# A state space layer: tiles and order of the decays, and the rows of the step product

## The chip, the cores and the metric

The kernel runs on one core of a Trainium2 chip. The metric is the device time of one execution in microseconds (us). The profile shows one execution on that core. Its engines are TensorE (PE; its weight loads are PEld), VectorE (DVE), ScalarE (ACT), GpSimd (POOL) and SyncE (SP, which here issues DMAs). "q" behind an engine's name is its sequencer.

## The reference, cut to what matters

The model has four layers of a token mixer and a channel mixer on an input of 4 x 64 x 128 x 128 floats. The change lies in the mixer of the third layer alone, a state space model (Mamba) over 64 x 128 positions of 128 values, cut here to its core:

```python
xs = silu(conv(xi))                       # D_INNER = 128 channels, 16384 positions a batch entry
x_dbl = einsum('bld,ed->ble', xs, x_proj_w)
dt, Bm, Cm = x_dbl[..., :4], x_dbl[..., 4:20], x_dbl[..., 20:]
dt = softplus(einsum('blr,dr->bld', dt, dt_proj_w) + dt_proj_b)
A = -exp(A_log)                           # 128 channels x 16 states
def step(h, t):
    dt_t, B_t, C_t, x_t = t
    h = exp(dt_t[:, :, None] * A) * h + (dt_t * x_t)[:, :, None] * B_t[:, None, :]
    return (h, einsum('bds,bs->bd', h, C_t))
y = (scan(step) + xs * D) * silu(z)
```

An output projection, a two-layer GELU network and the residual follow.

## The kernel before

The layer is the function `l2_conv`. Positions are cut into 64 chunks of 512 positions for two batch entries: `chunks` holds two groups of 32. A chunk n has T = 32 **units**, 16 for each batch entry b; unit t works on 128 rows (two states of 64 channels) x 512 positions:

- `decay(t)` (L2824, ACT) makes da = exp(dt * A) in a ring of five SBUF tiles;
- `spread(t)` (L2834, PE), for each pair of units, spreads a row of B over the partitions of a PSUM bank (bs), and `inputs(t)` (L2868, DVE) multiplies it by dx = dt * x. There are four banks for this, and `spread` must wait until the scan that used its bank is done;
- `one_state(t)` runs the scan (L2876, DVE), then multiplies the result by C (gs, L2881, POOL);
- `summed(t)` (L2890 and L2892, PE) adds two units' gs into py.

Units 16 and 17 of each chunk stand **apart**: their da goes into a PSUM bank and POOL makes their input (L2862).

While chunk n is scanned, the following chunks are prepared and the last one is finished. All this is written into one list of turns by hand, and the engines' order is the order of the list (`manual_schedule`); each engine works in order. In turn t the list has first the decay of unit t + 3, then `spread` of t + 3 (where that is even), POOL's input of t + 5, the loads of C, `inputs` of t + 1, `one_state` of t, then the other steps put at turn t, and last `summed` of t - 5 in every second turn. Counted within a chunk, the steps that matter below are:

| turn | step |
|---|---|
| 24 to 28 | `conv` (PE, L2621), `conv_out` (ACT, L2633) for the next chunk |
| 30, 31, 1 | `gate_in` (PE, L2639), `gate_out` (ACT, L2642), `silu` (ACT, L2648, two table loads) |
| 30 to 6 | `norm` of a later chunk: `scale` (ACT, L2541), `centre` (PE, L2547), `square` (ACT, L2550 and L2551, turn 4), `mean2` (PE, L2556, turn 5), `root` (ACT) |
| 7, 8 | `bcr` (PE, L2654): 100 rows: three times the 32 rows of B and C, then the four step rows |
| 9 | `bcr_out` (ACT): copies to bt (96 rows, L2658), bc (64 rows, L2659), r (the four step rows, L2660); `c_out`, the DMA of bc to memory (cd) |
| 10 to 13 | `minus` (PE, L2669) and `part` (ACT, L2675), twice; `back` (PE, L2575) and `kept` (ACT, L2581) of `norm` |
| 9 to 14 | `project_out` (PE, L2753), `projected` (ACT, L2756) |
| 15 | `steps` (PE, L2680): dt_proj times r |
| 16 to 18 | `parts` (ACT, L2684 and L2685), `exp`, `one_more` (L2688 to L2693, which makes `less`), `log` (L2696) |
| 18 to 23 | four products on POOL (`lost` L2699 to `scaled` L2716) and the DMAs that lay out dt and dx (L2708) |
| 18 to 22 | `layer1` (PE, L2761) and `hidden` (ACT, L2766), for b = 0 at 18 and 19, for b = 1 at 21 and 22 |
| 24 | `gelu` (ACT, L2771, two table loads) |
| 28 to 33 | `layer2` (PE, L2777 to L2780) and `put` (ACT, L2787) |

Every four chunks, `statistics` is added: sixteen DVE instructions (L2495) at turns 7 to 22, a merge on POOL (turn 24), ACT's root (L2511, turn 26) and POOL's refinement (turn 28), which the `scale` of the next chunk waits for.

## Time and profile before

| | |
|---|---|
| median of 3 runs | 10706.98 us (10702.95 to 10707.34) |
| the profiled execution | 10710.25 us, span 10708.5 us, mean granted PE clock 0.774 |
| the layer's scans (L2876) | first start 5839.5 us, last start 9713.0 us of the span (its waits included) |
| stretch 5840 to 9714 us | PE 3392.8, DVE 3693.8, ACT 3172.6, POOL 3508.0 us busy of 3874.0; clock 0.89; DMA 0.49 |
| one scan, one input product | 1271 ns, 677 ns |
| one decay, one product by C | 715 ns, 1272 ns |

A line of the groups names the source line, the engine, the operation, what it writes and reads with shapes, how often; behind the bar its busy time and the mean of one, then how long the engine stood idle just before it and who ended that. "<-" points to what is read or waited for. A line of the timeline gives start and duration, in brackets the idle time before it and what ended it. A line of the waits gives the waiting engine and line, who it waited for, the total in us, how often, and the longest. A line of the table of stretches gives the stretch, its length, the busy time and number of instructions of each engine asked for, the clock that PE was granted (1.00 is full), the busy share of the DMA engines and GB/s. Successive DVE instructions overlap by about 0.09 us.

### The profile page before, as it was taken

To read this page: it belongs to the slowest core of one execution; us is meant where nothing else is said; L and a number is where in the kernel's file an instruction comes from. 1 tells how busy PE (TensorE), PEld (TensorE's weight loads), DVE (VectorE), ACT (ScalarE), POOL (GpSimd) and SP (SyncE) were. 2 spreads that over 40 slices of the span, in tenths; PEclk is the share of its full clock that TensorE was granted. 3 is DMA by queue.
4 is the path that set the end of the run, shared out by engine and by line. 5 is a ranking of instruction groups with operands and counts; after the bars stand their busy time and mean duration, and the time that the engine had idled before them with its cause. 6 is when DMAs were issued, how large, how long until landed. Compare 5 with 4: busy or idle time off the path is not lost. (4 is left out here: it accounts for less than half of the span.)

```text
span 10708.5 us, 115288 instructions
## 1 busy us (share of the span) xinstructions
PE 6421.0 (60%) x33010; PEld 3761.6 (35%) x33010; DVE 9037.8 (84%) x14995; ACT 7129.8 (67%) x10685; POOL 6791.7 (63%) x6142
## 2 busy tenths in 40 slices
PE   7888686000000000029997888888888888887664
PEld 5665454000000000028885333333333333335342
DVE  7577746999999999987774999999999999996555
ACT  4245443788886777655653888888888888885443
POOL 1000025899996777515553989899999999983322
PEclk8888798555555555559997888888889888888887
DMA  6322246111111222121111544445454454543544
GB/s 198 115 39 53 72 161 160 51 57 59 57 57 58 75 75 75 63 59 52 56 49 51 129 122 123 124 120 130 120 127 123 123 130 120 129 115 108 185 151 164
DMA packets 806496, 1080.38 MB, mean 101 GB/s; under 512 B 245612, under 2 KB 462926, under 8 KB 792270
## 3 DMA queue, kind: packets, MB, share of 16 engines
q1 hardware_dynamic: 761918, 946.59, 31.4%
q0 software_dynamic: 34368, 124.14, 3.5%
q8 instruction: 266, 4.36, 0.2%
q14 instruction: 392, 3.21, 0.1%
q10 hardware_dynamic: 9552, 2.08, 0.1%
HBM read 699.16 MB, written 255.91 MB: 89 GB/s over the span
## 5 line engine op out<-in xcount | busy, mean ns | idle before, releaser
L2881 POOL TENSOR_TENSOR gs<-hist,cc 128x512 f32<-128x512 f32 x2048 | 2569.9, 1272 | 274.5 <-DVE hist L2876 203.7
L2876 DVE TENSOR_TENSOR_SCAN hist<-da,state,bs 128x512 f32<-128x512 f32 x1860 | 2360.8, 1271 | 50.8 <-ACT da L2824 49.2
L1752 PE MATMUL pm<-ident,m 128*1 128x128 f32 x1 | 0.4, 372 | 2812.9 <-DMA pk<-spare 2812.9
L2868 DVE TENSOR_TENSOR bs<-dx,bs 128x512 f32<-128x512 f32 x1920 | 1300.3, 677 | 165.1 <-PE bs L2834 115.4
L1509 POOL TENSOR_TENSOR diff<-key 128x2048 f32<-128x2048 f32 (+11 forms) x364 | 1384.2, 3860 | 81.7 <-DVE key L1514 75.9
L2824 ACT ACTIVATE da<-dt,am 128x512 f32<-128x512 f32 x1920 | 1294.3, 715 | 36.8 <-DVE hist L2876 28.4
L2892 PE MATMUL py<-gs,both 128*64 128x512 f32 x4096 | 1210.0, 671 | 0.4 <-POOL gs L2881 0.2
L1752 PEld LDWEIGHTS pm<-ident,m 128*1 128x1 f32 x1 | 0.1, 79 | 2813.0 <-issue 2813.0
L1507 ACT COPY low<-key 128x2048 f32<-128x2048 f32 (+11 forms) x364 | 627.5, 1724 | 314.2 <-DVE key L1514 276.9
L1561 ACT ACTIVATE back<-turned 128x2048 int32<-128x2048 int8 (+6 forms) x546 | 626.1, 1165 | 308.9 <-DVE rank L1572 294.1
L1570 DVE COPY_PREDICATED rank<-back,rank 128x2048 int16<-128x2048 int32 (+6 forms) x546 | 787.8, 1478 | 19.3 <-ACT keep L1565 6.2
L1514 DVE TENSOR_TENSOR key<-low,key 128x2048 f32<-128x2048 f32 (+11 forms) x364 | 744.5, 2045 | 12.4
L1513 DVE TENSOR_TENSOR key<-low,key 128x2048 f32<-128x2048 f32 (+11 forms) x364 | 749.2, 2058 | 2.4 <-ACT low L1507 2.4
L1510 ACT ACTIVATE turned<-diff 128x2048 int8<-128x2048 f32 (+11 forms) x364 | 600.4, 1699 | 7.9 <-POOL diff L1509 7.9
L1555 POOL TENSOR_TENSOR both<-rank 128x1280 int32<-128x1280 int32 (+5 forms) x156 | 381.1, 2443 | 298.8 <-DVE rank L1572 170.8
L2303 PE MATMUL pe<-ew,xg 128*128 128x128 f32 x4096 | 509.9, 278 | 0.0
L2303 PEld LDWEIGHTS pe<-ew,xg 128*128 128x128 f32 x4096 | 495.2, 194 | 22.0 <-issue 3.9
L1031 POOL DMA_DIRECT2D state<-zz x16 | 18.5, 1156 | 763.0 <-DVE zz L1021 349.3
L1576 POOL TENSOR_TENSOR rank<-both,rank 128x256 int32<-128x256 int32 (+10 forms) x312 | 423.5, 1379 | 117.5 <-DVE rank L1570 89.4
L2834 PE MATMUL bs<-bt,pick 96*128 96x512 bf16 x960 | 394.8, 411 | 123.6 <-DVE hist L2876 120.9
L2761 PE MATMUL pa<-o,f 128*128 128x256 f32 x1024 | 362.5, 515 | 101.4 <-ACT gl L2766 81.6
L2892 PEld LDWEIGHTS py<-gs,both 128*64 128x64 f32 x4096 | 214.2, 142 | 594.0 <-issue 247.7
(860 smaller groups left out, 18030.7 us busy)
## 6 DMA issues: line engine op xcount, KB each, us to landing
cc<-cd SPq DMA_DIRECT2D x1024, 256.0 KB
xt<-state SPq DMA_DIRECT2D x64, 1024.0 KB
dt<-w SPq DMA_DIRECT2D x512, 128.0 KB
dx<-up SPq DMA_DIRECT2D x512, 128.0 KB
xo<-state SPq DMA_DIRECT2D x128, 256.0 KB
state<-xo POOLq DMA_DIRECT2D x128, 256.0 KB, 3.3
xl<-in_L_ffn_weight SPq DMA_DIRECT2D x32, 1024.0 KB
tk<-in_x SPq DMA_DIRECT2D x32, 512.0 KB
```

The source lines that it names most:

```text
L1507: nc.scalar.copy(c, l)
L1509: nc.gpsimd.tensor_sub(d, lo[part], hi[part])
L1513: nc.vector.tensor_tensor(lo[part], c, hi[part], ALU.min)
L1514: nc.vector.tensor_tensor(hi[part], c, hi[part], ALU.max)
L1561: nc.scalar.activation(m, sv[part], AF.Relu)
L1570: nc.vector.copy_predicated(l, m, h)
L2303: T.matmul(w["pe"][:, j, :], w["xg"][:, q, j, :], ew[:, q, :], start=False, stop=(j == 3 and q == E - 1))
L2824: nc.scalar.activation(da, x_["dt%d" % b][:, s % 2, :], AF.Exp, scale=am[:, s : s + 1])
L2868: nc.vector.tensor_mul(live["db", t], x_["dx%d" % b][:, s % 2, :], live["bs", t - s % 2])
L2876: nc.vector.tensor_tensor_scan(h, live.pop(("da", t)), live.pop(("db", t)), 0.0 if first else state[b][:, s : s + 1], ALU.mult, ALU.add,)
L2881: nc.gpsimd.tensor_tensor(gs, h, live.pop(("cc", t)), ALU.mult)
L2892: nc.tensor.matmul(x_["py%d" % b][h * H : h * H + H], both, live.pop(("gs", t - 1 + h)), start=False, stop=(s == S - 1),)
```

## The change

- `dtw`, the weights of the step product, gets 3N + R = 100 rows instead of R = 4: a memset to zero, and the DMA of the four true rows into the last ones.
- `bcr_out` makes two copies instead of three: bc takes all 100 rows, r is gone. `steps` multiplies all 100 rows of bc by the 100 rows of `dtw`; the first 96 meet zeros.
- The ring for da gets eight tiles instead of five.
- Decays of units that do not stand apart are issued five turns ahead instead of three, and still first in their turn. Those of the two units apart stay at three.

```diff
-        dtw = load("dtw", [R, D], prm["dt_proj_wT"])
+        dtw = cp.tile([3 * N + R, D], F32, name="dtw")
+        nc.vector.memset(dtw, 0.0)
+        nc.sync.dma_start(dtw[3 * N :], prm["dt_proj_wT"])
...
                 nc.scalar.copy(tile_of(x_, "bt", [3 * N, 2, L], dt=BF16), ps[0 : 3 * N])
-                nc.scalar.copy(tile_of(x_, "bc", [2 * N, 2, L], bufs=1), ps[0 : 2 * N])
-                nc.scalar.copy(tile_of(x_, "r", [R, 2, L], bufs=1), ps[3 * N : 3 * N + R])
+                nc.scalar.copy(tile_of(x_, "bc", [3 * N + R, 2, L], bufs=1), ps[0 : 3 * N + R])
...
-                    nc.tensor.matmul(pu[:, b, :], dtw, x_["r"][:, b, :], start=True, stop=True)
+                    nc.tensor.matmul(pu[:, b, :], dtw, x_["bc"][:, b, :], start=True, stop=True)
...
-            da = bank(t, t % 2) if apart(t) else sb.tile([P, L], F32, name="da", bufs=5)
+            da = bank(t, t % 2) if apart(t) else sb.tile([P, L], F32, name="da", bufs=8)
...
-                if 0 <= t + 3 < units:
+                if 0 <= t + 5 < units and not apart(t + 5):
+                    decay(t + 5)
+                if 0 <= t + 3 < units and apart(t + 3):
                     decay(t + 3)
```

## The prediction

> **What bounds the kernel now.** The change lies in one layer. Its scan line L2876 runs from 5840 us to 9714 us (first and last start in the view of that line), 64 chunks of 32 units, about 60.5 us a chunk. In the table of stretches VectorE is the busiest engine there:

> ```profile
> 7000.00:7500.00 500.00, 438.30 (x1741) 186.91 (x1740) 478.00 (x562) 412.01 (x622) 452.86 (x457) 0.89 0.50 125
> ```

> Columns: PE, PE loads, DVE, ACT, POOL busy, granted clock, DMA. DVE lacks 22 us of 500. Its waits over the layer:

> ```profile
> DVE bs L2868 <- PE bs L2834: 115.4, 110, 3.2
> DVE hist L2876 <- ACT da L2824: 50.5, 49, 3.1
> ```

> So 166 us wait for PE or ACT, and that is all the change can win. Next the DVE timeline, which shows where. The waits repeat every four chunks (statistics cover four), some 242.3 us: 3.06 us for da at unit 5 and 1.29 us at unit 10 of the first chunk (A), 1.98 us at A's unit 22, 1.47 and 1.26 us at unit 26 of the second and third (B, C), 0.2 to 0.4 us elsewhere; about 10.4 us in all, beside 231.9 us of DVE work.

> ```profile
> 8882.48 1.28 DVE L2876 TENSOR_TENSOR_SCAN hist<-da,state,bs 128x512 f32<-128x512 f32 x1 [3.05 <-ACT da L2824]
> ...
> 8890.95 0.69 DVE L2868 TENSOR_TENSOR bs<-dx,bs 128x512 f32<-128x512 f32 x1 [1.29 <-PE bs L2834]
> ...
> 8895.00 0.70 DVE L2868 TENSOR_TENSOR bs<-dx,bs 128x512 f32<-128x512 f32 x1 [0.40 <-PE bs L2834]
> ...
> 8913.68 0.69 DVE L2868 TENSOR_TENSOR bs<-dx,bs 128x512 f32<-128x512 f32 x1 [1.98 <-PE bs L2834]
> ```

> Why is PE late? Following PE and ACT in time through chunk B gives one unbroken loop: bcr product (PE, ends 7013.69), three copies (ACT, to 7016.67), minus to steps (PE, 7016.72 to 7025.48), parts to hidden(0) (ACT, 7025.58 to 7035.14), layer1(1) to spread(26) (PE, to 7041.06), layer2 (PE, to 7057.56), put, silu, square (ACT, to 7065.5), mean2, dself, spread(10), bcr. It takes 59 us, DVE's own chunk 56.9. The loop, not the number of da tiles, is the bound.

> PE's clock belongs to it. Cut into stretches of 3.41 us, the granted clock is 1.00 or 0.50, nothing between:

> ```profile
> 7018.84:7022.25 3.41, 3.41 (x32) 1.00 0.42 121
> 7022.25:7025.66 3.41, 3.41 (x11) 1.00 0.50 109
> 7025.66:7029.08 3.42, 3.34 (x8) 0.51 0.24 72
> 7029.08:7032.49 3.41, 3.41 (x15) 0.99 0.35 82
> 7032.49:7035.90 3.41, 1.29 (x6) 1.00 0.00 0
> 7035.90:7039.32 3.42, 3.42 (x8) 0.51 0.61 153
> ```

> A stretch with PE busy under some 45% (1.29 us) is followed by one at half clock. The second line is fully busy and is followed by half clock too; 1.98 us of it are the steps product L2680, which uses 4 of 128 rows. Over the layer, all 44 full-clock stretches that steps share with at most 0.42 of other PE work were followed by half clock, the 15 with 0.53 or more of other work by full clock. I read: four rows don't count as work. In chunk A this half clock makes layer1(0) 3.78 us instead of 1.99 and the product behind it 1.98 instead of 1.08, and so the 1.98 us wait at unit 22.

> **The change, part by part.**

> One copy less. The groups (busy us, mean ns, idle before and its releaser) show that the number of rows doesn't set a copy's time:

> ```profile
> L2669 PE MATMUL pa<-bt,minus_i 64*64 64x512 bf16 (+1 forms) x256 | 77.7, 383 | 58.8 <-ACT r L2660 58.2 <-ACT bt L2675 0.6
> ...
> L2658 ACT CAST bt<-pa 96x1024 bf16<-96x1024 f32 x64 | 64.5, 1007 | 226.2 <-PE pa L2654 226.2
> L2660 ACT COPY r<-pa 4x1024 f32<-4x1024 f32 x64 | 64.4, 1006 | 1.5
> L2659 ACT COPY bc<-pa 64x1024 f32<-64x1024 f32 x64 | 64.3, 1005 | 0.0
> ```

> So bc with 100 rows takes 1.005 us, r's 1.006 us goes, and the DMA to cd leaves as before. PE's minus waited 0.86 us a chunk for r (58.2 us in all); that goes, as project_out before it ends 0.86 us earlier. Next late is spread(18), which needs scan 14: in B it stood at 7023.18, scan 14 ends 7022.45, so 0.7 us arrive; 0.86 in A, 0.5 in C (7324.26 against 7323.72), 0.2 in D, the chunk with statistics. From there ACT and PE run behind it without a gap, so the gain goes through to unit 26.

> Steps over 100 rows. Duration: the bcr product (128 rows, 100 columns) needs 1.88 us for its four at full clock (7312.89), steps 1.98: taken as equal, bounds -0.1 and +0.2 us a chunk (the load, 230 against 191 ns, overlaps). The clock effect no row shows directly: between 0 (rows don't matter) and the whole half-clock stretch. I take the whole, since bcr with 128 rows counts. Then layer1(0) and its follower in A save 2.7 us, and the 1.98 us wait goes.

> Decays five ahead in eight tiles. Order on ACT: decay(t+5) now stands before turn t's other work. Its tile is free after scan t-3, before after scan t-2: no new wait. Of every pair of fixed ACT steps the number of decays between is the same, so no other ACT step gets earlier; only da does. So the 3.06 us at unit 5 go, but A's square is still done at 7430.70 (three decays and silu before it, as now), mean2, dself and spread(10) follow, and unit 10 waits 3.06 + 1.29 = 4.35 instead. Worth: 0. Around the two units whose decays stay at three ahead, turns 11 and 12 lose theirs and 13 and 14 have two: 1.24 us more ACT work between kept and parts, against 1.59 us of ACT waiting there now. Hidden, with 0.25 us to spare; without that cover 0.7 us a chunk. decay(32) is issued at turn 27, two earlier, and needs dt by DMA. At the start of the layer da began 2.94 us after the DMAs' first issue (5832.66 to 5835.60); in B dt is issued at 7042.42, ACT comes there at 7046.9, 1.6 us to spare. Were it late, conv_out, scale and put(0) are queued behind, and put(0) waits 1.67 us for PE anyway.

> Once: memset of dtw (a 128x128 one takes 165 ns, L2387) ahead of its DMA on SP's queue, with the remaining constants and the first xt behind: 0 to 1 us. The first decay waits for dt ahead of conv_out in the fill: 0 to 2.5 us, less 1.0 us of r's copy there. Taken as 0.

> **The sum.** Chunk B in DVE's own time, 0 where unit 10's product starts (7011.80): scan 14 ends at 10.65 (7022.45); spread(18) then takes 0.33 and steps 1.98, so steps end at 13.0; parts to hidden(0) are 9.6 us of ACT (7025.58 to 7035.14), to 22.65; layer1(1) to spread(26) are 4.2 us at full clock (6976.31 to 6980.50 in A), to 26.9. DVE comes to unit 26 at 27.83 (7041.10 less the 1.47 of waiting): no wait. But PE idles 2.2 us before layer1(1); where that falls into one 3.41 us stretch (some 55% of positions) the next is at half clock, spread(26) ends at 28.6, and DVE waits 0.8. So per four chunks: 231.9 of DVE, 4.1 for A's unit 10 (statistics chain, tied to D's scan 14, 44 us long), 0.3 at unit 12, 0.55 x 0.8 x 3 = 1.3 at unit 26 of A to C, 0.9 at unit 10 of B to D (0.3 each, between 0 and 1.2, from the 0.18 and 0.41 there now). Sum 238.5 against 242.3: 3.8 us, by 15.5 groups 59 us. The profiled execution took 10710.25 us (span 10708.5), 3.3 above the median; less 59 that is 10651, and on the median's scale **10648 us**.

> **Rivals.** Forecast, 10648 (10635 to 10665): 0.45.

> (1) Rows don't count for the clock: A's unit 22 still waits 1.2 of its 1.98, so 2.6 us a group, 40 us: **10667**. For it: the 96 added rows meet zero weights. 0.21.

> (2) The clock takes the gain back. The changes from half to full clock in bcr (7012.0, 7196.4, 7254.4, 7373.8) lie 17 and 35 steps of 3.41 us apart, and the groups follow at 242.3 us, 71 steps; after a disturbed group of 243.4 the next took 241.5. Work that starts earlier is at half clock for longer, so half of each gain is lost at each such place, and 71 steps could hold: **10707**. Against it: A and D would have a fully busy stretch 3.41 us sooner once they start 0.7 us earlier. The step below is 70, 238.9 us, near my sum. 0.12. [...]

> (3) The lead pays too: the 3.06 us go and nothing replaces them, 47 us more, **10601**. Against it the square's fixed time. 0.08. [...]

> (4) Slower. PE, now ahead, waits for DVE in turns 24 to 33 (0.2 to 0.55 us before a spread today), and where a 3.41 us stretch there falls under 45% two at half clock follow: 3.4 us of PE on the way to put, silu, square. In two of four chunks that is 6.8 x 15.5 = 105 us: **10753**. It decides from 1.9 us of idle in one stretch; the largest in that part is now 1.76. 0.14.

> Faster by over 0.2% (21 us, about what a measurement tells from no change): 0.45 + 0.21 + 0.08 = 0.74; within: 0.12; slower: 0.14. The range 10600 to 10707 takes in the forecast, (1), (2) and (3), and leaves out (4), 0.14.

> **What would show it.** Right: no L2660; PE no longer waits 0.86 at L2669; DVE's wait for da near 0 and its unit 10 waits near 4 us once in four chunks; full clock behind steps and no wait at unit 22; groups at 238 to 240 us. Wrong: half clock behind steps (1); groups at 242.3 (2); unit 10 of A waiting under 2 us (3); ACT's parts starting later than steps' end, or DVE waits longer than now at units 26 to 10 (4).

## The result and the profile after

The changed kernel takes **10656.87 us** (median of 6 runs, 10646.97 to 10671.12) beside 10707.96 us for the kernel before (6 runs, 10702.95 to 10714.69): a ratio of 0.9954, 95% interval 0.9942 to 0.9965, or 49 us less. The forecast was 10648 us, 59 us less.

The profiled execution is the fastest of its six (10646.97 us, span 10645.2 us), so its span is 63.3 us shorter, more than the medians say. 6.1 us of that lie ahead of the layer (SP issues its first load at 5739.55 us, 5745.60 us before), 0.8 us in the fill, 56.3 us between the first and the last scan (3818.2 us beside 3874.5).

The table of stretches of the changed kernel, the same 500 us as before (columns: PE, PE loads, DVE, ACT, POOL, clock, DMA): DVE lacks 18 us where it lacked 22.

```profile
7000.00:7500.00 500.00, 432.02 (x1767) 184.46 (x1767) 481.76 (x568) 413.13 (x627) 461.40 (x459) 0.91 0.49 124
```

Its waits: the line for da, 50.5 us before, is gone, and the wait of the input products for PE is no smaller, 120.0 us beside 115.4.

```profile
DVE bs L2869 <- PE bs L2835: 120.0, 85, 4.6
```

The DVE timeline shows why, at unit 10 of the first chunk of a group (A): one wait of 4.46 us, where 3.05 us for da and 1.29 us for PE stood.

```profile
8844.33 0.70 DVE L2869 TENSOR_TENSOR bs<-dx,bs 128x512 f32<-128x512 f32 x1 [4.46 <-PE bs L2835]
...
8848.29 0.70 DVE L2869 TENSOR_TENSOR bs<-dx,bs 128x512 f32<-128x512 f32 x1 [0.32 <-PE bs L2835]
```

The groups of the layer: two copies of 1.01 us, `minus` (L2670) no longer waits (0.7 us in all, 58.2 before), and the step product over 100 rows takes 625 ns, not 638.

```profile
L2681 PE MATMUL pa<-bc,dtw 100*128 100x512 f32 x252 | 126.3, 625 | 0.0
...
L2670 PE MATMUL pa<-bt,minus_i 64*64 64x512 bf16 x252 | 76.6, 383 | 0.7 <-ACT bc L2661 0.7
...
L2661 ACT COPY bc<-pa 100x1024 f32<-100x1024 f32 x63 | 63.7, 1010 | 0.0
L2660 ACT CAST bt<-pa 96x1024 bf16<-96x1024 f32 x63 | 63.5, 1008 | 222.9 <-PE pa L2656 222.9
```

PE's clock in stretches of 3.41 us (PE busy, clock): the first holds all four of the step product and 3.10 us of PE work, and full clock follows.

```profile
7060.82:7064.23 3.41, 3.10 (x9) 1.00 0.46 111
7064.23:7067.64 3.41, 2.64 (x11) 1.00 0.19 69
```

From the first scan to the last, 6 of 72 full-clock stretches with more than 0.3 us of steps are followed by half clock; before, 46 of 76. Of those that hold the whole product (over 1.85 us of it), none of 35 is; before, all 43 were.

From the DVE timelines of this kernel and those of the experiments comes one table: us a group of four chunks (from the first scan of chunk 4 to that of chunk 60, 14 groups, one execution each), and in it the waits for da, at units 1 to 12 of A, at the same units of the other chunks (B to D), at unit 22, at units 26 and 28, and the rest (other units and DMA).

| kernel | group | da | A to 12 | B–D to 12 | 22 | 26, 28 | rest |
|---|---|---|---|---|---|---|---|
| before | 242.5 | 3.2 | 1.8 | 0.5 | 2.0 | 2.8 | 0.6 |
| changed | 239.5 | 0.0 | 4.7 | 0.4 | 0.0 | 2.6 | 0.9 |
| lead alone | 242.3 | 0.0 | 4.9 | 1.0 | 1.6 | 3.0 | 0.8 |
| copy and rows | 238.9 | 3.1 | 1.4 | 0.5 | 0.0 | 1.9 | 1.1 |
| copy alone | 240.9 | 3.5 | 1.6 | 0.4 | 2.5 | 0.7 | 1.3 |
| rows alone | 241.1 | 3.0 | 1.8 | 1.0 | 0.0 | 2.8 | 1.2 |
| 36 rows | 240.6 | 3.5 | 1.7 | 0.6 | 0.2 | 2.4 | 1.1 |
| changed, statistics early | 236.7 | 0.0 | 0.2 | 0.9 | 0.0 | 3.4 | 1.5 |
| changed, layer1(1) late | 244.8 | 0.0 | 2.2 | 4.9 | 0.0 | 4.0 | 2.5 |
| changed, both of these | 242.7 | 0.0 | 0.9 | 4.4 | 0.0 | 2.9 | 3.5 |
| both of these without the lead | 243.1 | 0.6 | 0.7 | 2.4 | 0.0 | 6.6 | 1.2 |
| changed, log late | 238.4 | 0.0 | 4.7 | 2.0 | 0.0 | 0.1 | 1.0 |
| changed, statistics early, log late | 233.8 | 0.0 | 0.0 | 0.6 | 0.0 | 0.3 | 2.9 |
| statistics early, log late, without the lead | 234.4 | 0.1 | 0.0 | 0.6 | 0.0 | 0.4 | 2.8 |

Executions of one kernel differ by up to 32 us (2 us a group), so verdicts come from the ratios (each to the kernel before on the same chip; in us, that share of 10708), and the table says where the waits stand.

### The profile page after: what moved, and what is told of

Same layout as the page of the kernel before. It is cut to its first block, busy times and chain, and to the rows that moved or that the text cites. A ratio compares the mean times of both kernels' runs of the same rounds, so it can differ in the third digit from the quotient of the medians.

```text
span 10645.2 us, 115085 instructions
## 1 busy us (share of the span) xinstructions
PE 6292.9 (59%) x33010; PEld 3711.6 (35%) x33010; DVE 9020.6 (85%) x14996; ACT 7065.7 (66%) x10621; POOL 6798.6 (64%) x6142
## 5 line engine op out<-in xcount | busy, mean ns | idle before, releaser
L2893 PE MATMUL py<-gs,both 128*64 128x512 f32 x4096 | 1176.7, 654 | 0.1
L1572 DVE COPY_PREDICATED rank<-back,keep 128x1152 int16<-128x1152 int32 (+21 forms) x234 | 381.6, 1631 | 8.0
```

The source lines that it names most:

```text
L2893: nc.tensor.matmul(x_["py%d" % b][h * H : h * H + H], both, live.pop(("gs", t - 1 + h)), start=False, stop=(s == S - 1),)
```

## The experiments

### The change taken apart

**The lead alone**: the last hunk and the eight tiles, on the kernel before. The step rows are copied into rows 96 to 99 of bc, and there is no tile r.

```diff
+                nc.scalar.copy(x_["bc"][3 * N :], ps[3 * N : 3 * N + R])
+                    nc.tensor.matmul(pu[:, b, :], dtw[3 * N :], x_["bc"][3 * N :, b, :], start=True, stop=True)
```

> The lead alone: decays five turns ahead in eight tiles; three copies and a step product over four rows as before (the step rows are copied into the last rows of the bc tile instead of a tile of their own, so that the eight tiles fit). My theory: nothing, 10708 us within 10; VectorE no longer waits for da at unit 5 of the first chunk of four (3.06 us before), but waits that much more at its unit 10 (4.35 us), and still at unit 22 (1.98 us). Rival, the lead pays: 47 us less, 10661 us, with the wait at unit 10 still 1.3 us.

Measured: ratio 1.0000 (0.9991 to 1.0009). Chunk A in its DVE timeline; no line for da is left, and what stood there is in the second line:

```profile
6213.33 0.69 DVE L2870 TENSOR_TENSOR bs<-dx,bs 128x512 f32<-128x512 f32 x1 [0.33 <-PE bs L2836]
...
6229.09 0.70 DVE L2870 TENSOR_TENSOR bs<-dx,bs 128x512 f32<-128x512 f32 x1 [4.44 <-PE bs L2836]
...
6233.12 0.70 DVE L2870 TENSOR_TENSOR bs<-dx,bs 128x512 f32<-128x512 f32 x1 [0.38 <-PE bs L2836]
...
6251.80 0.70 DVE L2870 TENSOR_TENSOR bs<-dx,bs 128x512 f32<-128x512 f32 x1 [1.98 <-PE bs L2836]
```

The lead is worth nothing, and rival (3) falls.

**All but the lead**: the change without its last two hunks.

> All but the lead: two copies, step product over 100 rows, decays three ahead in five tiles. My theory: all of the change's gain, 51 us less than before, 10657 us within 10; the da wait of 3 us stays, no wait at unit 22, full clock behind the step product. Rival, the lead pays 47 us: then this gives 4 to 12 us, about 10700 us.

Measured: 0.9954 (0.9940 to 0.9967), the ratio of the whole change. The wait for da is still there (50.5 us before), but PE's part is 61.0 us where the whole change has 120.0: the lead turns the one wait into the other.

```profile
DVE bs L2869 <- PE bs L2835: 61.0, 68, 3.0
DVE hist L2877 <- ACT da L2825: 48.2, 49, 3.1
```

**The copy alone**: two copies, but four rows in the product.

```diff
+                    nc.tensor.matmul(pu[:, b, :], dtw[3 * N :], x_["bc"][3 * N :, b, :], start=True, stop=True)
```

> The copy alone: two copies, bc with 100 rows, but the step product multiplies only the last four rows of it by the four rows of weights; decays as before. My theory: the copy gives the larger share, 2.6 us a group of four chunks or 40 us less, 10668 us, with half clock behind the step product in most chunks and 1.2 us of waiting left at unit 22 of the first chunk. Rival, the rows give all: 10700 us or more. Rival, the copy gives all and the clock nothing: 10657 us.

Measured: 0.9961 (0.9948 to 0.9975), 42 us less. The stretch with steps has 3.16 us of PE work, and here two at half clock follow:

```profile
8158.38:8161.79 3.41, 3.16 (x11) 1.00 0.48 123
8161.79:8165.20 3.41, 2.64 (x8) 0.50 0.22 52
8165.21:8168.62 3.41, 3.41 (x9) 0.50 0.42 103
```

Half clock follows in 53 of 55 places. The wait at unit 26 shrinks (0.7 us a group, 2.8 before), and 0.6 to 1.2 us stand at unit 22 in 35 of the 56 chunks, not in A alone as expected.

**The rows alone**: 100 rows in the product, and the copy of r is still made, unread.

```diff
-                    nc.tensor.matmul(pu[:, b, :], dtw, x_["r"][:, b, :], start=True, stop=True)
+                    nc.tensor.matmul(pu[:, b, :], dtw, x_["bc"][:, b, :], start=True, stop=True)
```

> The rows alone: step product over 100 rows of bc, and the third copy, of the four step rows, is still made though nothing reads it; decays as before. My theory: full clock behind the step product in nearly all chunks, the wait of 1.98 us at unit 22 of the first chunk is gone, those at unit 26 of the second and third (1.47, 1.26 us) stay: 1 to 2 us a group, 15 to 30 less, about 10685 us. Rival, zero rows do not count for the clock: half clock as before, 10708 us. Rival, the copy gives nothing: 10657 us.

Measured: 0.9975 (0.9966 to 0.9984), 27 us less. All 38 full-clock stretches with the whole product are now followed by full clock (of those with more than 0.3 us of it, 4 of 74 by half), and the wait at unit 22 is gone:

```profile
8163.50:8166.91 3.41, 3.41 (x13) 1.00 0.61 132
8166.91:8170.32 3.41, 2.58 (x13) 1.00 0.22 77
```

So zero weights do not take the rows out of the count, and rival (1) falls. Copy and rows, 42 and 27 us alone, give 49 together; the intervals (14, 10 and 14 us to either side) do not tell that from a sum.

**36 rows**: as all but the lead, with the last 36 rows of bc and of `dtw` in the product.

> Two copies, decays three ahead, and the step product over the last 36 rows of bc, between the 4 and the 100 of the others. If any product over more than one group of 32 rows counts as work for the clock: full clock behind it as with 100 rows (half clock in some 6 of 64 places), 51 us less than before. If the clock goes by the share of rows: half clock as with 4 rows (50 of 52 places), some 42 less than before. The clock in the trace tells them apart, the time hardly.

Measured: 0.9955 (0.9941 to 0.9969). Half clock follows in 28 of 64 places, between both theories: the whole product with 1.02 us beside it is followed by full clock, 1.54 us of it with 1.04 beside by half.

```profile
8148.99:8152.40 3.41, 3.00 (x9) 1.00 0.31 75
8152.41:8155.82 3.41, 3.00 (x13) 1.00 0.35 105
8207.02:8210.43 3.41, 2.58 (x9) 1.00 0.10 26
8210.43:8213.84 3.41, 3.41 (x8) 0.50 0.56 154
```

### The waits that are left

**Statistics early.**

```diff
-                at(t0 + 7 + j, lambda j=j: stats(j))
-            at(t0 + 24, merge)
-            at(t0 + 26, root)
-            at(t0 + 28, refine)
+                at(t0 + 7 + j // 2, lambda j=j: stats(j))
+            at(t0 + 18, merge)
+            at(t0 + 20, root)
+            at(t0 + 22, refine)
```

> The changed kernel, with the sixteen statistics instructions two a turn (turns 7 to 14 in place of 7 to 22), merge, root and refinement at turns 18, 20 and 22 (24, 26, 28). Nothing is left out. My theory: the wait of some 4.4 us at unit 10 of the first chunk of four is the statistics chain coming late to scale and square; ten turns earlier it goes, but for 0.3 to 1 us: 3.6 to 4.3 us a group, 56 to 67 us less than the changed kernel, 107 to 118 less than before. Rival, the square is late for ACT's own decays and silu: as the changed kernel, 51 us less than before.

Measured: 0.9919 (0.9905 to 0.9933), 87 us less than before and some 38 less than the changed kernel. The chain in the changed kernel's ACT timeline: ACT waits for the merge and for the refinement just ahead of A, and the square comes late by these:

```profile
8818.93 0.22 ACT L2513 ACTIVATE rs<-v 128x16 f32<-128x16 f32 x1 [4.40 <-POOL v L2509]
...
8825.72 0.88 ACT L2543 ACTIVATE xn<-xt,nb,rs 128x128 f32<-128x128 f32 x2 [2.62 <-POOL nb L2525]
...
8837.41 0.59 ACT L2553 ACTIVATE sq<-pn 128x512 f32<-128x512 f32 x1
```

With the statistics early, ACT's waits for the merge and the refinement fall from 65.5 and 41.2 us in all to 13.9 and 1.9, and A waits 0.2 us to unit 12 (4.7), so the cause is shown. Part of the 4.5 us comes back at once: 0.8 at unit 26, 0.5 to unit 12 of B to D, 0.6 in the rest. My size, 56 to 67 us, was too large by that.

**layer1(1) behind the spread.**

```diff
-            at(t0 + 21, lambda: layer1(1))
-            at(t0 + 22, lambda: hidden(1))
+            at(t0 + 23, lambda: layer1(1))
+            at(t0 + 23, lambda: hidden(1))
```

> The changed kernel, with layer1(1) and hidden(1) at turn 23 (21 and 22), so that PE makes the spread for unit 26 before layer1(1) and not behind it. My theory: the waits at unit 26 (2.6 us a group, 0.6 to 1.9 each) are PE's in-order queue: layer1(1) waits for ACT's hidden(0), and the spread behind it. They go: 30 to 40 us less than the changed kernel, 80 to 90 less than before. Rival, the loop from the bcr product through layer1, layer2, put and square to the next bcr bounds the group whatever stands first: the waits move to units 10 and 12 and the time is as the changed kernel's, 51 less than before.

Measured: 1.0030 (1.0020 to 1.0040), slower than before. Both theories left out what it was moved past: the product with dself, which waits for DVE's y. PE's timeline shows layer1(1) behind it, and conv then waits for hidden(1) to free the PSUM tile; ACT waits for layer1 229.6 us in all (78.4 before this move).

```profile
9060.52 1.12 PE L2891 MATMUL py<-xs,dself 128*128 128x512 f32 x2 [1.97 <-DVE y L2749]
...
9062.81 1.89 PE L2762 MATMUL pa<-o,f 128*128 128x256 f32 x8
9066.36 1.13 PE L2623 MATMUL pa<-xn,wconv 64*128 64x512 f32 x4 [1.66 <-ACT gl L2767]
```

The unit 26 wait goes to unit 28, and unit 10 waits 1.0 to 1.6 us in most chunks: the waits moved to unit 10 as the rival had it, and grew, which neither theory had. **Both moves** together:

> The changed kernel with both moves, statistics early and layer1(1) behind the spread. My theory: both waits go, a group takes 231.9 us of VectorE and 1 to 2 us of waiting, 233 to 234 us: 90 to 105 us less than the changed kernel, 140 to 155 less than before. Rival, the loop bounds the group: no more than the better of the two alone.

Measured: 0.9998 (0.9989 to 1.0007), far from the 140 to 155 us expected. The loss of the one takes the gain of the other. The same **without the lead**:

> Both moves, with two copies and the step product over 100 rows, but without the lead: decays three turns ahead in five tiles. My theory: the da wait of 3 us came from ACT standing behind the late statistics, so with these early there is none to win and this takes as long as with the lead, within 10 us. Rival, the lead pays once the chain is early: 15 us or more longer than with it.

Measured: 0.9993 (0.9984 to 1.0002), as with it. But where the product with dself holds PE back, this says little on the lead; the pair below says more.

**Log behind hidden(0)**: PE's idle time ahead of layer1(1) is made shorter at its source, and nothing on PE is moved.

```diff
-            at(t0 + 18, log, lost)
+            at(t0 + 18, lost)
+            at(t0 + 19, log)
```

> The changed kernel with ACT's log behind hidden(0) and nothing else. My theory: of the 2.6 us a group at unit 26 two thirds or more go: 25 to 40 us less than the changed kernel, 75 to 90 less than before. Rival, the loop through PE, ACT and DVE brings the waits back elsewhere: 51 less than before.

Measured: 0.9922 (0.9909 to 0.9936), 84 us less than before, some 34 less than the changed kernel. PE waits 54.4 us for hidden(0) ahead of layer1(1), 116.3 in the changed kernel. The waits at unit 26 fall to 0.1 us a group; 1.6 us come back to unit 12 of B to D.

**Statistics early and log late:**

> The changed kernel with the statistics early and with ACT's log behind hidden(0) (turn 19) and not ahead of it (turn 18), so that PE's idle time before layer1(1) is 0.95 us shorter. My theory: the waits at unit 26 (3.4 us a group with the statistics early) are hidden(0) coming late, and two thirds or more of them go: 35 to 50 us less than with the statistics early alone, 120 to 140 less than before. Rival, they move to another unit, as when layer1(1) was put later: 87 less than before.

Measured: 0.9879 (0.9864 to 0.9894), 130 us less. The input products wait 21.1 us for PE in the whole profile, where the changed kernel has 120.0:

```profile
DVE bs L2870 <- DMA dx<-up: 65.2, 18, 44.6
...
DVE bs L2870 <- PE bs L2836: 21.1, 31, 3.0
```

What is left at this line is the arrival of dx by DMA: 44.6 us in one wait ahead of the first scan, which the kernel before has too (45.6), and 20.6 us in 17 later ones.

**Statistics early and log late, without the lead**, three turns and five tiles:

> The same two moves (statistics early, log behind hidden(0)) with two copies and the step product over 100 rows, but decays three turns ahead in five tiles. My theory: the lead is worth nothing here either, as long as with the lead within 10 us. Rival: with the other waits gone the lead is worth 15 us or more.

Measured: **0.9866** (0.9851 to 0.9881), 143 us less, 10570.63 us median. It waits for da 0.1 us a group with five tiles. The two intervals overlap: the lead is worth nothing here, and this, the best version found, does without it.

## Why the prediction was right, step by step

- **The lead, 0.** Right: 1.0000 alone, no difference with the other edits. The 3.05 us became 4.46 at unit 10, forecast 4.35. (Before, ACT waits for da tiles too, 28.4 us in all for the ring and 7.3 for the banks of the units apart; but at most 0.2 us of it, once, stands just ahead of A's unit 5, so it isn't the tiles that unit 5 waits for.) ACT comes late to decay and square by the same chain of statistics, so once that is early the da wait is gone with five tiles too.
- **The copy, 0.86 us a chunk.** Right: `minus` waits for nothing, and alone it gives 42 us (40 in rival (1)).
- **The rows and the clock.** Right: full clock behind steps, no wait at unit 22; 27 us alone.
- **Unit 26, "0.55 x 0.8 x 3 = 1.3".** Mis-sized: 2.6 us a group. Count, in the changed kernel, the half-clock stretches that reach into the 8 us ahead of unit 26: in 18 of the 56 chunks none and no wait; in 22 one, and 15 of these wait 0.4 to 0.9 us, 7 under 0.2; in 16 two, and 15 of these wait 1.6 to 1.9 us. So 38 of 56 have at least one (0.68, forecast 0.55), but the larger error, the step that failed, is "the next is at half clock, spread(26) ends at 28.6": a second one follows, as I had reckoned only in rival (4). Four stretches and the wait, chunk 8 (layer1(1) starts at 6348.65):

```profile
6344.02:6347.43 3.41, 1.90 (x8) 1.00 0.12 26
6347.43:6350.84 3.41, 2.19 (x5) 0.50 0.19 67
6350.85:6354.26 3.41, 3.41 (x8) 0.50 0.37 90
6354.26:6357.67 3.41, 3.41 (x14) 1.00 0.16 37
```

```profile
6355.59 0.69 DVE L2869 TENSOR_TENSOR bs<-dx,bs 128x512 f32<-128x512 f32 x1 [1.70 <-PE bs L2835]
```

  Half clock follows the stretch in which PE idles; the next, at half clock, is not full either (2.19 us), and only behind the third (3.41 us) is the clock full again. The first was busy for 1.90 us, 56% of it: the prediction's bound of some 45% for a fall was too low as well.
- **Unit 10 of B to D, 0.9.** 0.4 measured.
- **The sum.** 238.5 forecast, 239.5 measured over 14 groups: 0.3 more in A, 1.3 more at unit 26, 0.5 less in B to D. The other waits, 0.9 us, stand in no term of the sum; DVE's own part was 1.1 us smaller (239.5 less 8.7 of waits is 230.8, not 231.9), and that the two cancel is luck. The gain is 3.0 us a group, 42 us; the other 14 us of the 56.3 are at the ends of the layer (5.0 in the first four chunks, 9.0 from chunk 60), where I had the same 3.8 us a group. So it is in part luck that the total comes near 59 us in this execution; by the ratio it is 49.
- **Rival (2)** held for a while: chunks 11 to 17 start 241.9 to 242.4 us after those four before them (71 steps are 242.3), with 1.7 to 1.8 us at unit 26 of every second chunk; then the group leaves 71 steps. Two half-clock stretches give part of the gain back, but do not hold it.
- **Rival (4)** did not come: PE does wait longer for DVE (220.0 us at the spread, 120.9 before), but DVE's waits from unit 26 to unit 10 of B to D, which should have grown by it, did not: 2.6 us a group at units 26 and 28 (2.8 before), 0.4 at units 1 to 12 of B to D (0.5 before). Two half-clock stretches did come, ahead of unit 26, where PE waits for ACT's hidden(0).

## What to carry to other kernels

A wait that is removed by issuing earlier comes back at the next instruction that hangs on the same late source (3.05 us for da at unit 5 went, and unit 10 waited 4.46 us where it had 1.29): follow both to the source (here the statistics) before you count the first. Moving an instruction in an engine's list costs what it is moved past, as layer1(1) behind dself showed; shortening the work ahead of it was worth some 34 us, moving it cost some 80. Where a clock follows the work before it, as PE's did here, price the stretch after next too: in chunk 8 one stretch of 1.90 us was followed by two at half clock.

## What was not expected of the hardware

The 3.41 us are those of the trace's own clock: between the first and the last scan it was granted in 301 spells before and 235 after, each at 1.00 or 0.50, and each lasted a multiple of 3.413 us. On the fall, in the kernel before: of the full-clock stretches without steps, all 95 with under 1.54 us of PE work (the 45%) were followed by half clock, 9 of the 20 with 1.54 to 1.94 us, and none of the 688 with more. In the changed kernel it was 73 of 74, 37 of 62 and none of 715.
